# One level of Strassen for five float32 weight products, in two passes with the result in DRAM between

## The chip, the cores and the metric

One core of one Trainium2 chip. The metric is the time of one execution on the device in microseconds (us): 3072.22 before, the median of three runs (3071.91 to 3073.43). The clock given for a run is the mean granted TensorE clock of its profiled execution.

## The reference

Two graph layers over 128 graphs of 64 nodes with 768 features: 8192 rows, 64 tiles of 128 rows (two graphs each), all in float32. Cut to what matters:

```python
# layer 0: three weight products
h = relu(layernorm(x))
ctx = adj @ (h @ Wadj.T + badj) / deg + adj.T @ (h @ Wrev.T + brev) / rdeg + h @ Wself.T + bself
x = x + ctx + rel                 # rel: counts of relations, times small tables
# layer 1: two weight products, attention with 6 heads, a gate
h = relu(layernorm(x))
hw   = einsum('bni,hio->bhno', h, W)
attn = softmax(mask(leaky(src(tanh(hw)) + dst(tanh(hw)).T)))
feat = elu(attn @ hw + b)
gate = sigmoid(h @ H_w.T + H_b)
x = x + gate * feat + (1 - gate) * h
```

The five products with 768 x 768 weights, Wadj, Wrev, Wself, W and H_w, are nearly all of the arithmetic.

## The kernel before

One pass over the 64 tiles; layer 0 of tile t is interleaved with layer 1 of tile t - 1 and the attention of tile t - 2. The parts that the change replaces (cuts marked with `# ...`):

```python
    def stage_c(t):                                     # layer 0: three products in one PSUM sum
        # ...
        for s in (2, 0, 1):
            for kb in range(KB):                        # KB = 6 blocks of 128
                for hf in range(2):
                    nc.tensor.matmul(pc[:, hf, :HALF], S1T[t][:, kb, s, :],
                                     ws[s][:, kb, hf * HALF : (hf + 1) * HALF],
                                     start=(n == 0), stop=False)
        # ... counts times table, add to x, layernorm

    def stage_d(t):                                     # layer 1: two products
        # ... six transposes of h
        def product(w):
            p = psb.tile([P, 2, 512], F32, name="pb")
            for kb in range(KB):
                for hf in range(2):
                    nc.tensor.matmul(p[:, hf, :HALF], h1t[:, kb, :],
                                     w[:, kb, hf * HALF : (hf + 1) * HALF],
                                     start=(kb == 0), stop=(kb == KB - 1))
        ph = product(wh)
        # ... tanh on ScalarE; ph + bias on VectorE; two products with w_src, w_dst on GpSimd
        pg = product(wg)

    for t in range(NT + 2):
        # ...
        stage_e(t - 2)
        stage_c(t)
        stage_a(t + 1)
        stage_f(t - 2)
        # ...
        stage_d(t - 1)
```

Of the kernel before, what the change touches and what calls it, by code (L numbers as in the profile page):

```python
# [22 lines left out]
def kernel(  # L23
# [35 lines left out]

    nc = tc.nc  # L60
# [4 lines left out]
    KB = D // P  # L65
    H, DO = w_src.shape
# [3 lines left out]
    CT = 2  # L70
    NCH = NT // CT
# [3 lines left out]
    NROW = NCNT + 5  # L75
    W = DO + 1
    assert GT == 2 and N == 64 and DO == P and H == KB and NROW <= P and NT % CT == 0
# [5 lines left out]
    work = ctx.enter_context(tc.tile_pool(name="work", bufs=2))  # L83
    small = ctx.enter_context(tc.tile_pool(name="small", bufs=3))
    psb = ctx.enter_context(tc.tile_pool(name="psb", bufs=3, space=bass.MemoryType.PSUM))
    pss = ctx.enter_context(tc.tile_pool(name="pss", bufs=2, space=bass.MemoryType.PSUM))


    X, AI = {}, {}

    def load_x(t):
        if t < NT:
            X[t] = work.tile([P, D], F32, name="xt", bufs=4)
            nc.sync.dma_start(X[t], xf[t * P : (t + 1) * P, :])

    def load_adj(c):
        if c < NCH:
            AI[c] = work.tile([P, CT, 2, N], I32, name="ai", bufs=3)
            for d, src in ((0, adj), (1, adj_t)):
                nc.sync.dma_start(  # L100
                    AI[c][:, :, d, :],
                    src[c * CT * GT : (c + 1) * CT * GT].rearrange("(t g) i j -> (g i) t j", g=GT),
                )

    load_x(0)
    load_adj(0)
    load_x(1)


    ws = [const.tile([P, KB, D], F32, name=f"w{s}") for s in range(3)]  # L110
    wh = const.tile([P, KB, D], F32, name="wh")
    wg = const.tile([P, KB, D], F32, name="wg")
    tab = const.tile([NROW, D], F32, name="tab")
    bb = const.tile([P, DO], F32, name="bb")
    hbb = const.tile([P, D], F32, name="hbb")
    wsd = const.tile([P, 2, D], F32, name="wsd")
# [8 lines left out]
    et = const.tile([P, NREL], F32, name="et")  # L125
    nc.scalar.dma_start(et, e_t)
    wrt = work.tile([P, 2, D], F32, name="wrt", tag="s1", bufs=1)
    nc.scalar.dma_start(wrt[:, 0, :], wr_t)
    nc.scalar.dma_start(wrt[:, 1, :], wrr_t)
    for i, v in enumerate((br, brr, badj, brev, bself)):  # L130
        nc.scalar.dma_start(tab[NCNT + i : NCNT + i + 1, :], row(v, 1))
    for w, src in ((ws[2], wself_t), (ws[0], wadj_t), (ws[1], wrev_t), (wh, w_cat), (wg, hw_t)):
        for k in range(0, KB, 2):
            nc.scalar.dma_start(  # L134
                w[:, k : k + 2, :],
                src[k * P : (k + 2) * P, :].rearrange("(k p) n -> p k n", p=P),
            )
    nc.scalar.dma_start(bb, row(b_att, P))
    nc.scalar.dma_start(hbb, row(hb, P))
    nc.scalar.dma_start(wsd[:, 0, :], row(w_src, P))  # L140
    nc.scalar.dma_start(wsd[:, 1, :], row(w_dst, P))
# [9 lines left out]
    for g in range(GT):  # L151
# [3 lines left out]
    blkb = const.tile([P, P], BF16, name="blkb")  # L155
    nc.vector.tensor_copy(blkb, blk)
# [3 lines left out]
    vals = const.tile([P, NV, N], BF16, name="vals")  # L160
    nc.gpsimd.iota(vals, pattern=[[1, NV], [0, N]], base=1, channel_multiplier=0,
                   allow_small_or_imprecise_dtypes=True)
    rs_, pbds = [], []
    for i in range(2):
        a = const.tile([P, CT, 3, N], F32, name=f"r{i}")
        for k in range(CT):
            nc.vector.tensor_copy(a[:, k, 2, :], idc)
        rs_.append(a)
        p = const.tile([P, H, P], F32, name=f"pbd{i}")
        nc.gpsimd.memset(p, 0.0)  # L170
        pbds.append(p)


    ids = const.tile([P, NV], F32, name="ids")
    nc.gpsimd.iota(ids, pattern=[[1, NV]], base=1, channel_multiplier=0,
                   allow_small_or_imprecise_dtypes=True)
    es = const.tile([P, 2, NCNT], F32, name="es")
    nc.vector.memset(es, 0.0)
    for d in range(2):
        nc.vector.tensor_mul(es[:, d, d * NV : (d + 1) * NV],  # L180
                             et[:, d * NB + 1 : (d + 1) * NB], ids)
    pt = psb.tile([P, 2, 512], F32, name="pb")
    for hf in range(2):
        for d in range(2):
            nc.tensor.matmul(pt[:NCNT, hf, :HALF], es[:, d, :],
                             wrt[:, d, hf * HALF : (hf + 1) * HALF],
                             start=(d == 0), stop=(d == 1))
    nc.vector.tensor_copy(tab[:NCNT, :].rearrange("p (a b) -> p a b", a=2),
                          pt[:NCNT, :, :HALF])


    def norm_relu(src, name, bufs):

        st = small.tile([P, 2, 6], F32, name="st")
        for i in range(2):
            nc.vector.bn_stats(st[:, i, :], src[:, i * HALF : (i + 1) * HALF])  # L196
        mv = small.tile([P, 2], F32, name="mv")
        nc.vector.bn_aggr(mv, st.rearrange("p a b -> p (a b)"))
        ve = small.tile([P, 1], F32, name="ve")
        nc.vector.tensor_scalar(ve, mv[:, 1:2], EPS, None, op0=OP.add)  # L200
        rs = small.tile([P, 1], F32, name="rs")
        nc.gpsimd.tensor_tensor(rs, ve, mhalf, op=OP.pow)  # L202
        h = work.tile([P, D], F32, name=name, bufs=bufs)
        nc.vector.tensor_scalar(h, src, mv[:, 0:1], 0.0, op0=OP.subtract, op1=OP.max)
        nc.scalar.activation(h, h, AF.Copy, scale=rs)  # L205
        return h

    AB, CNT, RR = {}, {}, {}

    def prep_adj(c):  # L210

        if c >= NCH:
            return
        ai = AI[c]
        af = work.tile([P, CT, 2, N], F32, name="af", bufs=1)
        nc.vector.tensor_copy(af, ai)
        AB[c] = work.tile([P, CT, 2, N], BF16, name="ab")
        nc.gpsimd.tensor_copy(AB[c], af)
        cnt = CNT[c] = work.tile([P, CT, NROW], F32, name="cnt")
        nc.vector.tensor_reduce(cnt[:, :, NCNT : NCNT + 2], af, AX.X, OP.add)  # L220
        dc = small.tile([P, CT, 2], F32, name="dc")
        nc.vector.tensor_scalar(dc, cnt[:, :, NCNT : NCNT + 2], 1.0, None, op0=OP.max)
        rc = small.tile([P, CT, 2], F32, name="rc")
        nc.vector.reciprocal(rc, dc)
        nc.vector.tensor_mul(cnt[:, :, NCNT + 2 : NCNT + 4], cnt[:, :, NCNT : NCNT + 2], rc)
        nc.vector.memset(cnt[:, :, NCNT + 4 : NCNT + 5], 1.0)


        ds = pss.tile([P, CT, 2, N], F32, name="ps")
        nc.tensor.matmul(ds, blkb, AB[c], start=True, stop=True)  # L230
        rd = work.tile([P, CT, 2, N], F32, name="rd", bufs=1)
        nc.vector.tensor_scalar(rd, ds, 1.0, None, op0=OP.max)
        nc.vector.reciprocal(rd, rd)
        r = RR[c] = rs_[c % 2]
        for d in range(2):
            nc.vector.tensor_mul(r[:, :, 1 - d, :], af[:, :, d, :], rd[:, :, d, :])

    H0, CT_T, S1T, H1 = {}, {}, {}, {}
    HS, TG, SD, L, PB = {}, {}, {}, {}, {}

    def stage_a(t):

        if t >= NT:
            return
        c, k = divmod(t, CT)
        H0[t] = norm_relu(X[t], "h0", 1)
        for d in range(2):
            eq = work.tile([P, NV, N], BF16, name="eq", bufs=1)
            nc.vector.tensor_tensor(  # L249
                eq, AB[c][:, k, d, None, :].to_broadcast([P, NV, N]), vals, op=OP.is_equal)  # L250
            nc.vector.tensor_reduce(CNT[c][:, k, d * NV : (d + 1) * NV], eq, AX.X, OP.add)  # L251

    def stage_b(t):

        if t >= NT:
            return
        c, k = divmod(t, CT)
        pt = pss.tile([P, P], F32, name="ps")
        nc.tensor.transpose(pt[:NROW, :], CNT[c][:, k, :], ident)  # L259
        CT_T[t] = work.tile([NROW, P], F32, name="cntT")  # L260
        nc.scalar.copy(CT_T[t], pt[:NROW, :])

        s1 = S1T[t] = work.tile([P, KB, 3, P], F32, name="s1", bufs=1)
        for q in range(KB // 2):
            ps = psb.tile([P, GT, 512], F32, name="pb")
            for i in range(2):
                kb = 2 * q + i
                for g in range(GT):
# [3 lines left out]
                                     RR[c][s, k].rearrange("p s n -> p (s n)"),  # L272
# [5 lines left out]
    def stage_c(t):  # L278

        if t >= NT:  # L280
            return
        pc = psb.tile([P, 2, 512], F32, name="pb")
        n = 0
        for s in (2, 0, 1):
            for kb in range(KB):
# [12 lines left out]
    def stage_d(t):  # L298

        if not 0 <= t < NT:  # L300
            return
# [157 lines left out]
```

## Time and profile before

| | before |
|---|---|
| time | 3072.22 us |
| TensorE busy | 2977.0 us, 97% |
| VectorE, ScalarE, GpSimd busy | 58%, 20%, 18% |
| chain of work that ended last | TensorE 95% |
| one tile in the steady stretch | 46.90 us, so 93.80 us a pair of tiles |

The last row is the distance between the starts of the layer-0 products of two tiles in the timeline (1011.33 and 1058.23 us). The busy time of that stretch; the columns are the stretch, its length, then busy us and instructions of PE, PEld, DVE, ACT and POOL, the granted clock, the DMA share and GB/s:

```profile
1011.33:1058.23 46.90, 46.31 (x178) 28.62 (x176) 35.72 (x41) 9.41 (x16) 8.87 (x9) 1.00 0.06 20
```

TensorE hardly rests (46.31 us busy of 46.90); the next busiest, VectorE, has a quarter of its time free. The other lines of this profile are in the prediction.

### The profile page before, as it was taken

How to read it: one execution, taken by the hardware profiler on the slowest of the kernel's cores; microseconds unless marked ns; L12 is line 12 of the kernel's file. 1: busy time of each engine (PE TensorE's matmuls, PEld its weight loads, DVE VectorE, ACT ScalarE, POOL GpSimd, SP SyncE). 2: the span in 40 equal slices, each digit the busy share in tenths (PEclk: the TensorE clock that was granted, in tenths of full speed). 3: DMA queues.
4: the chain of work that ended last, by engine and by line, in shares of the span. 5: the costliest groups of instructions: out<-in, count | busy, mean ns of one | idle time of the engine just before them, and what ended most of it. 6: DMA issues, size and time to landing. Idle time of an engine off the chain costs nothing.

```text
span 3070.0 us, 27575 instructions
## 1 busy us (share of the span) xinstructions
PE 2977.0 (97%) x11240; PEld 1839.7 (60%) x11240; DVE 1773.2 (58%) x2319; ACT 602.4 (20%) x961; POOL 561.4 (18%) x554
## 2 busy tenths in 40 slices
PE   5999999999999999999999999999999999999997
PEld 3666666666666666666666666666666666666664
DVE  8266555576555665555765556655557655566334
ACT  1112121121121121211211211212112112112121
POOL 1112122121121121221211211212212112112111
PEclk7999999999999999999999999999999999999998
DMA  5000000000000000000000000000000000000000
GB/s 207 1 23 23 12 23 21 13 23 12 23 22 12 23 23 13 23 21 12 23 13 22 22 11 23 23 13 23 21 12 23 15 21 23 11 23 23 11 16 16
DMA packets 41064, 70.18 MB, mean 23 GB/s; under 512 B 19941, under 2 KB 20069, under 8 KB 40938
## 3 DMA queue, kind: packets, MB, share of 16 engines
q1 hardware_dynamic: 35840, 54.54, 5.4%
q10 hardware_dynamic: 5098, 13.89, 1.2%
q8 instruction: 88, 1.44, 0.2%
q14 instruction: 38, 0.31, 0.0%
HBM read 43.24 MB, written 25.17 MB: 22 GB/s over the span
## 4 chain that ended last, share of the span: by engine, by line
PE 95%; ACT 2%; DMA 1%; issue 1%; DVE 0%; ACTq 0%; POOL 0%
PE pb L287 48%; PE pb L314 33%; PE pb L270 5%; PE pb L380 3%; PE pb L292 3%; PE ps L352 2%; ACT pT L376 1%; ACT h1t L308 1%; PE ps L375 1%; PE ps L307 1%; DMA wh<-in_w_cat_dram 0%; ACTq L134 0%; PE ps L259 0%; PE ps L230 0%; DMA wrt<-in_wr_t_dram 0%
## 5 line engine op out<-in xcount | busy, mean ns | idle before, releaser
L287 PE MATMUL pb<-w,s 128*128 128x384 f32 x4608 | 1496.8, 486 | 0.0
L287 PEld LDWEIGHTS pb<-w,s 128*128 128x128 f32 x4608 | 875.4, 190 | 610.5 <-issue 0.4
L314 PE MATMUL pb<-wh,h1t 128*128 128x384 f32 x1536 | 512.4, 490 | 18.7 <-ACT h1t L308 18.7
L314 PE MATMUL pb<-wg,h1t 128*128 128x384 f32 x1536 | 505.8, 486 | 0.0
L295 DVE TENSOR_TENSOR xt<-pb,xt 128x768 f32<-128x768 f32 x64 | 61.3, 958 | 752.3 <-PE pb L292 752.2
L314 PEld LDWEIGHTS pb<-wh,h1t 128*128 128x128 f32 x1536 | 286.6, 190 | 220.4 <-ACT h1t L308 33.8
L314 PEld LDWEIGHTS pb<-wg,h1t 128*128 128x128 f32 x1536 | 291.8, 190 | 203.5
L251 DVE TENSOR_REDUCE cnt<-eq 128x39 f32<-128x2496 bf16 x128 | 352.4, 2753 | 2.2
L376 ACT COPY pT<-ps 128x384 f32<-128x384 f32 x128 | 55.2, 482 | 1244.7 <-PE ps L375 1244.5
L323 POOL MEMSET hs<- 128x6 f32 x64 | 7.3, 113 | 1327.7 <-PE pb L380 1327.7
L249 DVE TENSOR_TENSOR eq<-ab,vals 128x2496 bf16<-128x2496 bf16 x128 | 186.5, 1457 | 3.3
L331 POOL TENSOR_TENSOR pr<-th,wsd 128x768 f32<-128x768 f32 x64 | 116.0, 1813 | 365.9 <-ACT th L321 365.9
L270 PE MATMUL pb<-r,h 64*128 64x192 f32 x1536 | 145.1, 336 | 7.5 <-ACT h L205 7.5
L270 PEld LDWEIGHTS pb<-r,h 64*128 64x128 f32 x1536 | 126.2, 190 | 31.0 <-issue 22.9
L274 ACT COPY s<-pb 128x768 f32<-128x768 f32 x192 | 140.0, 799 | 3.5 <-PE pb L270 3.5
L337 DVE TENSOR_TENSOR tg<-pb,hbb 128x768 f32<-128x768 f32 x64 | 61.3, 958 | 134.5 <-PE pb L314 134.5
L357 POOL MEMSET lm<- 128x384 f32 x64 | 26.7, 417 | 578.1 <-ACT pbd L365 578.1
L196 DVE BATCH_NORM_STATS2 st<-xt 128x6 f32<-128x384 f32 x256 | 127.2, 539 | 2.9 <-DMA xt<-in_x_dram 0.7
L202 POOL TENSOR_TENSOR rs<-ve,mhalf 128x1 f32<-128x1 f32 x128 | 107.6, 851 | 89.4 <-DVE ve L200 89.2
L380 PE MATMUL pb<-hs,pT 128*128 128x129 f32 x768 | 105.0, 287 | 18.6 <-ACT pT L376 18.6
L389 DVE TENSOR_SCALAR e<-f 128x768 f32<-128x768 f32 x64 | 120.7, 1886 | 2.2
L205 ACT ACTIVATE h<-h,rs 128x768 f32<-128x768 f32 x128 | 113.2, 931 | 44.2 <-POOL rs L202 44.1
(70 smaller groups left out, 2090.8 us busy)
## 6 DMA issues: line engine op xcount, KB each, us to landing
xt<-in_x_dram SPq DMA_DIRECT2D x64, 384.0 KB, 3.2
out_dram<-f SPq DMA_DIRECT2D x64, 384.0 KB, 2.6
w<-in_wself_t_dram ACTq DMA_DIRECT2D x3, 768.0 KB, 9.7
w<-in_wadj_t_dram ACTq DMA_DIRECT2D x3, 768.0 KB, 13.1
w<-in_wrev_t_dram ACTq DMA_DIRECT2D x3, 768.0 KB, 14.7
wh<-in_w_cat_dram ACTq DMA_DIRECT2D x3, 768.0 KB, 15.0
wg<-in_hw_t_dram ACTq DMA_DIRECT2D x3, 768.0 KB, 15.4
ai<-in_adj_dram SPq DMA_DIRECT2D x32, 64.0 KB, 1.9
```

The lines of the kernel that those rows point to most:

```text
L196: nc.vector.bn_stats(st[:, i, :], src[:, i * HALF : (i + 1) * HALF])
L202: nc.gpsimd.tensor_tensor(rs, ve, mhalf, op=OP.pow)
L205: nc.scalar.activation(h, h, AF.Copy, scale=rs)
L249: nc.vector.tensor_tensor(eq, AB[c][:, k, d, None, :].to_broadcast([P, NV, N]), vals, op=OP.is_equal)
L251: nc.vector.tensor_reduce(CNT[c][:, k, d * NV : (d + 1) * NV], eq, AX.X, OP.add)
L270: nc.tensor.matmul(ps[:, g, i * 3 * N : (i + 1) * 3 * N], H0[t][s, kb * P : (kb + 1) * P], RR[c][s, k].rearrange("p s n -> p (s n)"), star ...
L274: nc.scalar.copy(s1[:, 2 * q : 2 * q + 2].rearrange("p i s (g n) -> p g (i s) n", g=GT), ps[:, :, : 6 * N].rearrange("p g (x n) -> p g x n ...
L287: nc.tensor.matmul(pc[:, hf, :HALF], S1T[t][:, kb, s, :], ws[s][:, kb, hf * HALF : (hf + 1) * HALF], start=(n == 0), stop=False)
L314: nc.tensor.matmul(p[:, hf, :HALF], h1t[:, kb, :], w[:, kb, hf * HALF : (hf + 1) * HALF], start=(kb == 0), stop=(kb == KB - 1))
L331: nc.gpsimd.tensor_mul(to, th, wsd[:, s, :])
L380: nc.tensor.matmul(po[:, b, i * W : (i + 1) * W], pT[:, h, :], HS[t][:, h, :], start=True, stop=True)
L389: nc.vector.tensor_scalar(e, f, 0.0, None, op0=OP.min)
```

## The change

Strassen's algorithm multiplies two 2 x 2 block matrices with 7 block products in place of 8. Here the two tiles of a pair are the block rows, the halves of 768 the block columns. A pair needs 63 matmuls of 128x384 in layer 0 (72 before) and 42 in layer 1 (48 before). In return, sums of operand blocks (S1 to S4) are made on VectorE and GpSimd, and each result block collects several products by adds. The seven products are called P1 to P7. The sums of weights are kept in SBUF, where the kernel has its tiles, one layer's at a time; so layer 0 runs over all pairs first, writes its result to DRAM, and layer 1 runs after it. The intent was less work for the engine that bounds the kernel. The table product became bf16 in three parts in the same change. Names that recur below: h is a tile's normalised rows; pr and th are GpSimd's products for the attention logits and dg its last operand for them; PSUM, in tiles that the kernel calls banks, is where its products' sums stand until another engine reads them. Core of the diff, long parts cut:

```diff
-    work = ctx.enter_context(tc.tile_pool(name="work", bufs=2))
+    X1 = [dram.tile([2 * P, D], F32, name=f"x1_{p}") for p in range(NP)]
 ...
-        for s in (2, 0, 1):
-            for kb in range(KB):
-                for hf in range(2):
-                    nc.tensor.matmul(pc[:, hf, :HALF], S1T[t][:, kb, s, :], ...
+            mm("a", lambda: A1[p][:, :, 0], "11", True)
+            add(x0, 0, "a")
+            mm("c", lambda: A1[p][:, :, 1], "21", True)
+            counts("c", 0, 0)
+            add(x0, 0, "c")
+            mm("b", lambda: S1[p], "T1", True)
+            add(x1, 1, "b")
+            mm("a", lambda: S2[p], "T2", False)
+            add(x0, 1, "a")
+            mm("d", lambda: A22[p], "T4", True)
+            ...
+            mm("a", lambda: S3[p], "T3", False)
+            ...
+            mm("b", lambda: S4[p], "22", False)
 ... second pass
+        def norm(t):
+            h = H1[t] = work.tile([P, D], F32, name="h1", bufs=6)
+            nc.scalar.activation(h, X[t], AF.Relu, scale=mv1[:, t, 0:1], bias=mv1[:, t, 1:2])
+                    if s == 0:
+                        nc.scalar.copy(part(t, s, q), sums(b, s))        # P1, P5, P6, P4: copy on ScalarE
+        def add(t, s, q, b):
+                nc.vector.tensor_add(part(t, s, q), sums(b, s), part(t, s, q))
+        def gate(t):
+            ...
+            nc.gpsimd.tensor_add(HS[t][:, :, :DO], HS[t][:, :, :DO],     # bias, on VectorE before
+                                 bb[:, None, :].to_broadcast([P, H, DO]))
+            nc.gpsimd.tensor_add(X[t], X[t], H1[t])
+        def final(t):
+            ...
+            nc.gpsimd.tensor_sub(e, e, H1[t])
+            nc.vector.scalar_tensor_tensor(f, f, 0.0, e, op0=OP.max, op1=OP.add)
+            nc.vector.scalar_tensor_tensor(f, f, -1.0, Z[t], op0=OP.add, op1=OP.mult)
+            nc.vector.tensor_add(f, f, X[t])
+        for p in range(NP):
+            merged(main(p), before(p + 1) + behind(p - 1))               # 42 products, side steps between
```

## The prediction

> **What bounds the kernel now.** I read the page of the kernel before from the top: busy shares, chain, groups; then the busy time by stretches, the timeline of one steady tile and the one of the last tiles.
>
> ```profile
> PE 2977.0 (97%) x11240; PEld 1839.7 (60%) x11240; DVE 1773.2 (58%) x2319; ACT 602.4 (20%) x961; POOL 561.4 (18%) x554
> ...
> PE 95%; ACT 2%; DMA 1%; issue 1%; DVE 0%; ACTq 0%; POOL 0%
> ...
> L287 PE MATMUL pb<-w,s 128*128 128x384 f32 x4608 | 1496.8, 486 | 0.0
> ...
> L314 PE MATMUL pb<-wh,h1t 128*128 128x384 f32 x1536 | 512.4, 490 | 18.7 <-ACT h1t L308 18.7
> L314 PE MATMUL pb<-wg,h1t 128*128 128x384 f32 x1536 | 505.8, 486 | 0.0
> ```
>
> TensorE bounds it: 97% busy, 95% of the chain of work that ended last. The five weight products are 2304 + 1536 matmuls of 128x384, each recorded twice (4608, 2 x 1536), and take 1496.8 + 512.4 + 505.8 = 2515 us: 0.65 us each, 39 us of the 47 us per tile. So removing a matmul shortens the kernel, as long as the others keep up.
>
> ```profile
> 0.00:40.00 40.00, 8.15 (x20) 3.90 (x22) 36.65 (x54) 2.53 (x4) 9.29 (x17) 0.72 0.95 351
> ...
> 1000.00:2000.00 1000.00, 987.57 (x3753) 610.43 (x3752) 598.91 (x775) 200.99 (x321) 186.73 (x182) 1.00 0.06 19
> ```
>
> Busy time by stretches (columns: length, then PE, PEld, DVE, ACT, POOL busy). The first 40 us are start (weights at 351 GB/s, VectorE full); later PE is busy 987.57 of 1000. The full clock (1.00) is granted there.
>
> The costs I need for VectorE and GpSimd are in the groups and timelines:
>
> ```profile
> L251 DVE TENSOR_REDUCE cnt<-eq 128x39 f32<-128x2496 bf16 x128 | 352.4, 2753 | 2.2
> L249 DVE TENSOR_TENSOR eq<-ab,vals 128x2496 bf16<-128x2496 bf16 x128 | 186.5, 1457 | 3.3
> ...
> L331 POOL TENSOR_TENSOR pr<-th,wsd 128x768 f32<-128x768 f32 x64 | 116.0, 1813 | 365.9 <-ACT th L321 365.9
> ```
>
> ```profile
> 1041.08 1.81 POOL L391 TENSOR_TENSOR xt<-xt,h 128x768 f32<-128x768 f32 x1 [0.21 <-ACT h L205]
> 1041.36 1.95 DVE L389 TENSOR_SCALAR e<-f 128x768 f32<-128x768 f32 x1
> ...
> 3009.58 1.87 POOL L391 TENSOR_TENSOR xt<-xt,h 128x768 f32<-128x768 f32 x1 [1.08 <-ACT h L205]
> ...
> 3010.75 1.51 DVE L393 SCALAR_TENSOR_TENSOR f<-f,e 128x768 f32<-128x768 f32 x1 [0.97 <-ACT e L390]
> 3012.30 0.96 DVE L394 SCALAR_TENSOR_TENSOR f<-f,h 128x768 f32<-128x768 f32 x1
> ```
>
> Timeline columns: start, duration. The first VectorE op takes 1.95 us beside GpSimd; alone at the kernel's end it takes 0.56. The second, with two SBUF inputs, takes 1.51 against 0.96: it ends at 3012.26, 0.81 us after GpSimd ended at 3011.45.[...]
>
> [...]
>
> **The change, part by part.** The unit is a pair of tiles (32 pairs).
>
> *Removed.* Strassen takes 7 block products for 8: layer 0 has 3 x 7 x 3 = 63 matmuls per pair for 72, layer 1 has 42 for 48. 15 x 0.65 = 9.75 us a pair, 312 us in all. The table products become 8 bf16 matmuls (1.3 us) for 4 float32 ones (93.2/32 = 2.9 us): another 1.6 us a pair, 51 us, less about 10 for split transposes.
>
> *TensorE floor.* Layer 0 per pair: 63 x 0.65 = 41.0; operands 2 x 145.1/64 = 4.5; table 1.3; the rest 0.8: 47.6 us. Layer 1: 42 x 0.65 = 27.3; transposes 2 x 1.68 = 3.4; attention 2 x 1.64 = 3.3; the block product 1.4: 35.4 us. 32 x 83.0 = 2656 us, against 2977 busy now. If the rest hid, start and ends of some 110 us would give about 2770.
>
> *But the other engines now have the same work in less time, each stage with its own share*[...]. So I took the compiled order of each engine's instructions for one steady pair and added up durations from the groups.
>
> *Layer 0.* VectorE, from the last add of a pair: that add and the statistics 3.7 (of it some 1.9 waiting for GpSimd's power, which it now needs back), two statistics 1.0, degrees 0.4, reciprocal 1.75, add 0.55, r 0.5, conversions and statistics 2.8, then the four comparisons and counts 4 x (1.46 + 2.75) = 16.8, mixed with two adds (1.1) and small ones (1.1), and only then S3 and S1 of the next pair's first block (1.1). With gaps of 0.03 us that is about 31.7 us. The third block of operands can start on TensorE only when those two have freed a PSUM buffer (two buffers for all operands); TensorE gets there at 28.4 us. It waits some 3.3 us, and nothing gives it back, since the next pair starts from the same add: 47.6 + 3.3 = 50.9 us.
>
> *Layer 1.* GpSimd has, per pair, 12 operations of 1.81 us (four products for the logits, bias, x + h, e - h), two of 0.83, two sums of 0.9 and small ones: 22.6 of 35.4 us. VectorE 25 us, of which 9.2 have two SBUF inputs[...]. From the end of the first half's last product (P3): VectorE's final step of an older tile[...] (3.0), the add (0.55), tanh (0.9), then on GpSimd pr, h + b, th, h + b, pr, th, e - h at 1.81 and dg 0.85, with one VectorE op between (0.9): dg lands at about 18.9. TensorE wants it at 14.4: 4.5 us. Then the logits' PSUM is read only at 25.2, after VectorE operations that wait for GpSimd in turn, and the next transpose, which needs that buffer, waits 2.3 more. 35.4 + 6.8 = 42.2 us.[...]
>
> *Start, seam, end.* In pair 0, VectorE has counts, weight sums (9 x 1.26, contending with 8 us on GpSimd) and the table ahead; the table's matmul stops TensorE until about 80, and pair 0 ends near 112. Layer 1's first loads wait for all engines of pass 0, since the memory is used again: 4.7 MB at 351 GB/s are 13 us, sums after, so P5 starts some 25 us late. The last pair leaves logits, softmax and final steps, some 40 us.
>
> *Sum.* 112 + 30 x 50.9 + 43 (last pair, without preparations) + 25 + 25 (rest of layer 1's first pair) + 31 x 42.2 + 40 = 3080. The gain of 320 us goes to waits: 99 in layer 0, 210 in layer 1, the rest at start and seam.
>
> **The rivals.** (a) *TensorE remains the bound*, about 2770 to 2850: for it speaks the 70% mean load of VectorE in both passes, banks with one or two products between write and reuse, and the evident trouble taken over placing the steps. Against it speaks the compiled order: side steps don't stand where their numbers put them; the four counts come together, ahead of S3 and S1. (b) *The waits hold in layer 0[...]*: 38 us in layer 1, 3080 - 130 = 2950. Against it is the pair of timeline rows above, if only one of many operations. (c) *Worse*:[...] layer 1 takes 44 to 45 us: 3150. (d) *DRAM between the passes*: 50 MB more traffic, at the 384 KB in 3.2 us of the issues listed, prefetched: hidden; only the seam is paid.
>
> **Range and chances.** The sum is 3080. Ledgers of this kind count each wait once and fully, and (a) and (b) lie only below; I say 3055, range 2900 to 3160. Faster means under 3011, which needs (b) or most of (a): 0.33. Within 2% (3011 to 3134): 0.48. Slower: 0.19, from (c) and a longer start.
>
> **What would show it.** TensorE busy about 2650 us, some 86% of the span. Products of layer 0 (63 a pair) and layer 1 (42 a pair) at 0.65 us each. A pair every 51 us in the first half; PE's waits there name the third operand block, released by VectorE. In the second half a pair every 42 us, VectorE ops of 0.96 us lasting up to 2.7 us, PE waiting for dg and then for the logits' reader. A seam of some 25 us with an idle TensorE. I am wrong if TensorE is above 92% busy, if layer 1's pairs take under 38 us, or if the second half's two-input operations keep their 0.96 us.

The cut passages (marked) named mechanisms and figures that no run of this case shows; they stood behind my estimate of how much longer operations of VectorE and GpSimd get beside each other. No term of the sums goes with them: 35.4 + 6.8 = 42.2 us for layer 1 and 3080 us in all are as recorded. Only the reason for the 3.0 us of VectorE's final step is gone, and that the same sum came to 38 us without this lengthening. That is rival (b), lengthening that costs little; (c) is more of it. The 1.3 us for eight bf16 table products was an estimate, and the trace of the kernel after shows it: two take 0.33 us of TensorE's stream (650.53 to 650.86), so eight 1.32.

## The result, and the profile after

3037.38 us, the median of four runs (3035.43 to 3038.00), against 3072.82 us of the kernel before on the same chip. The ratio is 0.9884, 95% interval 0.9867 to 0.9901: 1.2% less, by the rule of 2% the same. (Ratios are the mean time of one kernel's fast runs over that of the other's of the same rounds, so not quite the ratio of the medians quoted.) The mean granted TensorE clock fell from 0.992 to 0.956. The result is correct.

TensorE lost 237 us of work (2977.0 to 2740.4), and the kernel only 35. The page of the kernel after, busy shares and chain:

```profile
PE 2740.4 (90%) x10360; PEld 1638.6 (54%) x10360; DVE 1970.5 (65%) x2999; ACT 752.5 (25%) x1251; POOL 1170.5 (39%) x1021
...
PE 40%; POOL 24%; DVE 19%; issue 11%; DMA 3%; ACT 3%; SPq 0%; ACTq 0%; POOLq 0%; DVEq 0%
```

GpSimd's work doubled, and what ended last hung on TensorE for 40% only. Three stretches: a pair of layer 0, the seam between the passes with the first pair of layer 1, a pair of layer 1 (columns as above):

```profile
613.90:663.30 49.40, 48.99 (x189) 28.32 (x188) 31.99 (x50) 6.75 (x12) 10.32 (x13) 1.00 0.11 35
...
1647.60:1715.10 67.50, 35.80 (x110) 21.50 (x110) 25.95 (x33) 12.38 (x19) 29.39 (x24) 0.75 0.41 144
2166.40:2207.70 41.30, 35.77 (x137) 22.47 (x136) 27.81 (x43) 16.68 (x27) 24.49 (x19) 0.92 0.12 40
```

Layer 0 is bound by TensorE: 48.99 of 49.40 us. Layer 1 isn't: 35.77 of 41.30, and its clock is 0.92. The waits of TensorE by name (us in total, times, longest):

```profile
PE pma L560 <- ACT hs L585: 160.7, 29, 5.9
PE pb L332 <- DVE s L352: 31.2, 30, 12.5
PE ps L531 <- DMA x<-x: 24.1, 1, 24.1
```

One wait makes up nearly all of layer 1's loss: 29 times 5.5 us, product P6 for ScalarE's copy of P1, which frees the PSUM bank that both use. The timeline of one steady pair shows why the copy is late (start, duration; in brackets idle time and what ended it):

```profile
2206.04 2.52 POOL L638 TENSOR_TENSOR pr<-th,wsd 128x768 f32<-128x768 f32 x1
2206.93 2.45 DVE L708 TENSOR_TENSOR f<-f,x 128x768 f32<-128x768 f32 x1
2207.69 2.10 PE L560 MATMUL pma<-bv,a 128*128 128x384 f32 x6
2208.52 2.43 POOL L649 TENSOR_TENSOR hs<-hs,bb 128x768 f32<-128x768 f32 x1
...
2212.69 1.74 POOL L649 TENSOR_TENSOR hs<-hs,bb 128x768 f32<-128x768 f32 x1
...
2218.07 1.80 POOL L705 TENSOR_TENSOR e<-e,h 128x768 f32<-128x768 f32 x1
...
2219.91 1.03 ACT L524 ACTIVATE h<-x,mv 128x768 f32<-128x768 f32 x1 [5.45 <-POOL e L705]
2220.84 0.46 ACT L585 COPY hs<-pma 128x384 f32<-128x384 f32 x1
...
2221.44 1.62 PE L560 MATMUL pma<-bvT,s 128*128 128x384 f32 x2 [5.52 <-ACT hs L585]
```

Read it from below. TensorE stood 5.52 us for the copy at 2220.84. The copy's input, P1, was there since 2209.79; yet ScalarE stood idle for 5.45 us and ran the copy only behind the normalisation h at 2219.91, which stood ahead of it and waited for GpSimd's e - h: the new h reuses the buffer which that operation reads. And e - h came last of seven long GpSimd operations in a row, from 2206.04 to 2219.87. So the wait called "copy of P1" is GpSimd's queue. The waits' view alone names ScalarE, which is 25% busy.

The matmuls after the wait take 1.62 us for two records, which take 0.81 elsewhere: from 2221.44 to 2225.00 the granted clock is 0.50, and in the stretch above it is 0.92. Where the same wait is only 2.23 us (next section, e2) the two records take 0.88. But in e6 (next section) two records take 1.49 us soon after a wait of only 2.01 us. So in these runs the length of the wait alone doesn't decide; what else does, no run shows.

Groups that answer to those of the prediction (busy, mean ns of one | idle before):

```profile
L308 DVE TENSOR_REDUCE cnt<-eq 128x39 bf16<-128x2496 bf16 x128 | 351.5, 2746 | 2.0
L638 POOL TENSOR_TENSOR pr<-th,wsd 128x768 f32<-128x768 f32 x64 | 138.2, 2159 | 13.5 <-ACT th L634 13.5
L649 POOL TENSOR_TENSOR hs<-hs,bb 128x768 f32<-128x768 f32 x64 | 131.0, 2047 | 0.0
L707 DVE SCALAR_TENSOR_TENSOR f<-f,z 128x768 f32<-128x768 f32 x64 | 124.7, 1949 | 0.1
L708 DVE TENSOR_TENSOR f<-f,x 128x768 f32<-128x768 f32 x64 | 110.8, 1731 | 0.1
```

The counts cost what they did. Two-input VectorE operations, 0.96 us in the kernel before, now average 1.95 and 1.73, and the GpSimd ones that meet them 2.05 to 2.16 for 1.81. In the timeline above both sides last longest where they overlap (2.45 beside 2.52 and 2.43 us): these collisions are real, as predicted; why they take time, no run shows.

### The profile page after: what moved, and what is told of

The parts are those of the page before. It is cut to its first block, busy times and chain, and to the rows that moved or that the text cites. A ratio compares the mean times of both kernels' runs of the same rounds, so it can differ in the third digit from the quotient of the medians.

```text
span 3035.0 us, 27842 instructions
## 1 busy us (share of the span) xinstructions
PE 2740.4 (90%) x10360; PEld 1638.6 (54%) x10360; DVE 1970.5 (65%) x2999; ACT 752.5 (25%) x1251; POOL 1170.5 (39%) x1021
## 3 DMA queue, kind: packets, MB, share of 16 engines
q8 instruction: 82, 1.34, 0.2%
## 4 chain that ended last, share of the span: by engine, by line
PE 40%; POOL 24%; DVE 19%; issue 11%; DMA 3%; ACT 3%; SPq 0%; ACTq 0%; POOLq 0%; DVEq 0%
PE pwa L376 8%; PE pma L560 7%; PE pwb L376 7%; PE pwd L376 6%; DVE cnt L308 5%; POOL pr L638 4%; POOL hs L649 4%; DVE eq L305 4%; POOL th L638 4%; POOL e L705 4%; PE pmc L560 4%; POOL s L362 2%; DVE st L142 2%; POOL rn L147 2%; POOL x L651 2%
## 5 line engine op out<-in xcount | busy, mean ns | idle before, releaser
L560 PE MATMUL pma<-bvT,s 128*128 128x384 f32 x768 | 331.6, 545 | 160.7 <-ACT hs L585 160.7
L376 PE MATMUL pwa<-bwT,s 128*128 128x384 f32 x1152 | 401.5, 493 | 0.0
L308 DVE TENSOR_REDUCE cnt<-eq 128x39 bf16<-128x2496 bf16 x128 | 351.5, 2746 | 2.0
L376 PEld LDWEIGHTS pwa<-bwT,s 128*128 128x128 f32 x1152 | 210.7, 190 | 141.6 <-issue 19.4
L332 PE MATMUL pb<-r,h 64*128 64x192 f32 x1536 | 178.6, 351 | 49.6 <-DVE s L352 31.2
L376 PE MATMUL pwb<-bwT,s 128*128 128x384 f32 x576 | 216.7, 505 | 0.0
L376 PE MATMUL pwb<-bw,s 128*128 128x384 f32 x576 | 201.3, 492 | 0.0
L376 PE MATMUL pwd<-bwT,a 128*128 128x384 f32 x576 | 201.2, 495 | 0.0
L376 PE MATMUL pwa<-bw,a 128*128 128x384 f32 x576 | 196.6, 489 | 0.0
L376 PE MATMUL pwc<-bw,a 128*128 128x384 f32 x576 | 191.0, 486 | 0.0
L560 PE MATMUL pmb<-bvT,s 128*128 128x384 f32 x384 | 146.6, 492 | 7.0 <-DVE s L545 7.0
```

Of the source, the lines that this page charges most:

```text
L308: nc.vector.tensor_reduce(CNT[p][:, k, d * NV : (d + 1) * NV], eq, AX.X, OP.add)
L332: nc.tensor.matmul(ps[:, g, i * 3 * N : (i + 1) * 3 * N], H0[t][s, kb * P : (kb + 1) * P], rts[p % 2][s, k].rearrange("p s n -> p (s n)"), ...
L376: nc.tensor.matmul(bank[b][:, :HALF], a()[:, q, s, :], bw[w][:, q, s, :], start=(first and q == s == 0), stop=(q == KH - 1 and s == 2), sk ...
L560: nc.tensor.matmul(bank[b, s][:, :HALF], a[p][:, q, :], bw[w][:, q, s, :], start=(first and q == 0), stop=(q == KH - 1), skip_group_check= ...
```

## The experiments

Four explanations of layer 1's 41.3 us a pair: (A) too few h buffers, (B) the length of GpSimd's queue, (C) the collisions, the longer durations of VectorE's and GpSimd's operations beside each other, (D) TensorE's own work. And one question beyond: what Strassen itself gives, and what the two passes cost. All runs were timed in three rounds (4 runs of each changed kernel; the kernel before took 3072.7 to 3073.1 us in each session); the pair is the mean distance of layer 1's pairs in the timeline over some 25 pairs. In the kernel after most pairs take 41.3 us and some 42.5, so the mean is 41.7. Classes follow the rule of 2%: the kernel after and e1 are the same as the kernel before, e6 is unclear, e7 to e9 are slower, the others faster.

| run | edit | us | ratio to before | pair of layer 1 | clock |
|---|---|---|---|---|---|
| after | | 3037.38 | 0.9884 | 41.7 | 0.956 |
| e1 | 8 h buffers | 3029.65 | 0.9861 | 41.4 | 0.969 |
| e2 | no bias add | 2924.55 | 0.9515 | 38.0 | 0.977 |
| e3 | bias add replaced by a free fill | 2953.89 | 0.9616 | 38.0 (steady) | 0.973 |
| e4 | e1, and bias on VectorE | 2977.27 | 0.9687 | 39.8 | 0.966 |
| e5 | bias add replaced by bound fills | 2971.76 | 0.9668 | 39.3 | 0.966 |
| e6 | bias on VectorE | 3015.02 | 0.9810 | 41.0 | 0.956 |
| e7 | layer 1 without Strassen | 3157.05 | 1.0274 | 45.7 | 0.965 |
| e8 | layer 0 without Strassen | 3194.56 | 1.0397 | 41.6 | 0.958 |
| e9 | neither with Strassen | 3314.40 | 1.0785 | 45.7 | 0.968 |
| e10 | second tile's heads earlier | 2987.55 | 0.9718 | 40.1 | 0.980 |
| e11 | e10 and e6 | 2949.97 | 0.9603 | 39.0 | 0.978 |
| e12 | e11 and 8 h buffers | 2937.36 | 0.9557 | 38.7 | 0.979 |

**e1: more h buffers.**

```diff
-            h = H1[t] = work.tile([P, D], F32, name="h1", bufs=6)
+            h = H1[t] = work.tile([P, D], F32, name="h1", bufs=8)
-            e = work.tile([P, D], F32, name="e")
+            e = work.tile([P, D], F32, name="e", bufs=1)
```

> Eight buffers for the normalised rows of layer 1 instead of six (and one instead of two for the exponentials, to make room). The changed kernel takes 3037 us and 41.3 us a pair in layer 1; TensorE waits 5.5 us a pair for ScalarE's copy of product P1, which stands behind a normalisation that waits for GpSimd (e - h) to give back a buffer. Theory A, the buffer count is the cause: the wait goes, 35.5 to 36.5 us a pair, 2860 to 2890 us. Theory B, GpSimd's chain to dg is the cause and the buffer only the place where it shows: the wait moves to dg, which lands 1.8 us sooner because one x + h leaves its way: 39 to 40 us a pair, 2965 to 3000 us, PE waiting for POOL dg.

3029.65 us (3028.17 to 3031.57): 8 us less. The wait that the trace of the kernel after names is gone, and others took its place:

```profile
PE ps L658 <- POOL dg L642: 104.9, 33, 11.8
PE ps L531 <- ACT a L542: 61.5, 29, 2.8
```

The buffer through which GpSimd's lateness reached TensorE was not its cause. A is out. B's forecast had the place right, dg, and the gain wrong: 8 us instead of 37 to 72.

**e2: no bias add.** The bias is zero in these inputs, so the result stays correct; this is an experiment and no kernel to keep.

```diff
-            nc.gpsimd.tensor_add(HS[t][:, :, :DO], HS[t][:, :, :DO],
-                                 bb[:, None, :].to_broadcast([P, H, DO]))
```

> GpSimd's two additions of the attention bias per pair are dropped (the bias is zero in these inputs, so the result stays right; in general it would be wrong). GpSimd loses 3.6 of 24.7 busy us a pair. Theory B (GpSimd's chain sets the pair): the pair falls by 3.6 us or a bit more[...]: 36 to 37.7 us, 2875 to 2925 us. If the buffer count, the evacuations or TensorE set it: within 0.5 us of 41.3, 3020 to 3040 us.

(The reason for the "bit more" is cut; no run shows it as a rule.)

2924.55 us (2920.22 to 2926.81), just within B's forecast, the pair (38.0) just above it: 113 us less for 64 operations of some 2 us on an engine that is 39% busy. The same place in the timeline:

```profile
2206.04 2.52 POOL L638 TENSOR_TENSOR pr<-th,wsd 128x768 f32<-128x768 f32 x1
...
2208.65 2.42 POOL L638 TENSOR_TENSOR th<-th,wsd 128x768 f32<-128x768 f32 x1
...
2214.76 1.81 POOL L703 TENSOR_TENSOR e<-e,h 128x768 f32<-128x768 f32 x1
...
2216.60 1.03 ACT L524 ACTIVATE h<-x,mv 128x768 f32<-128x768 f32 x1 [2.14 <-POOL e L703]
2217.53 0.46 ACT L585 COPY hs<-pma 128x384 f32<-128x384 f32 x1
...
2218.14 0.88 PE L560 MATMUL pma<-bvT,s 128*128 128x384 f32 x2 [2.23 <-ACT hs L585]
```

From the first product to the end of e - h GpSimd needs 10.53 us instead of 13.83: 3.30 less, and this pair is as much shorter (38.04 us for 41.34, from one first product to the next). TensorE's wait falls by 3.29. So GpSimd's work in that chain sets the pair, microsecond for microsecond. Whether by its time or by the collisions, the time alone doesn't say; the line at 2208.65 is taken up under e5.

**e3: a fill in place of the add.** A write of the same engine that reads nothing, meant to be about as long (it took 1.48 us, for 1.74 to 2.43 of the add; with one e buffer, as in e1, to make room for it).

```diff
-            nc.gpsimd.tensor_add(HS[t][:, :, :DO], HS[t][:, :, :DO],
-                                 bb[:, None, :].to_broadcast([P, H, DO]))
+            nc.gpsimd.memset(scr, 0.0)          # scr: 128 x 1660, read by nobody
```

> The same two additions are replaced by memsets of about the same length (1660 elements, some 1.8 us), which read no SBUF. GpSimd keeps its time[...]. If only GpSimd's time counts: 3025 to 3045 us, as the changed kernel. If [...] (VectorE's L706 to L708 last 1.25 to 1.95 us for 0.96): the pair falls by 1 to 2 us, 2975 to 3005 us.

(The cut clauses rest on a cause of the collisions that no run shows; the second forecast is for C as a large part.)

2953.89 us (2951.41 to 2960.16), 84 us less than after and below both forecasts. I first took this as the collisions' share of e2's gain. It isn't: the run failed as an experiment, as one line on the fill shows (duration min/median/max in ns, first and last start):

```profile
L651 POOL MEMSET scr<- x64: 1472/1482/1490, 1656.9 to 1814.8; 128x1660 f32 x64
```

The fill depended on nothing, so the scheduler moved all 64 to the start of layer 1. The steady pairs have none and last 38.0 us, as e2's; the 29 us between e2 and e3 are lost at the start.

**e4: e1 with the bias on VectorE.** The bias joins the multiplication that reads the attention's PSUM, as the reference has it.

```diff
-            nc.vector.tensor_mul(FF[t][...], po[:, :, :DO], ri.to_broadcast([P, HH, DO]))
+            for i in range(HH):
+                h = q * HH + i
+                nc.vector.scalar_tensor_tensor(FF[t][:, h * DO : (h + 1) * DO], po[:, i, :DO],
+                                               ri[:, i, :], bb, op0=OP.mult, op1=OP.add)
```

> Eight buffers as in the first run, and the bias is added by VectorE where it reads the attention out of PSUM (three operations of 128x128 with one SBUF input in place of one of 128x384), so that GpSimd no longer has it; right for any bias. VectorE gains about 1 us a pair. Theory B: dg lands 3.6 us sooner again, waits of 0 to 1.5 us are left, 35.5 to 37 us a pair, 2860 to 2905 us, some 5 to 7% under the kernel before. If VectorE is now the limit: 38 us or more a pair, above 2935 us.

2977.27 us (2974.17 to 2978.32): a miss for theory B; the other forecast (above 2935) came. TensorE's waits were for VectorE's read of the logits (67.5 us) and ScalarE's copy of a transposed block (45.4 us).

**e5: the fill again, bound to its place.**

```diff
-            nc.gpsimd.tensor_add(HS[t][:, :, :DO], HS[t][:, :, :DO], ...
+            nc.gpsimd.memset(HS[t][:, :, :DO], 0.0)
+            nc.gpsimd.memset(HS[t][:, :, :DO], 0.0)
+            nc.gpsimd.memset(HS[t][:, :HH, :DO], 0.0)
```

> Repeats the question of e3 properly. In e3 the write-only fill depended on nothing, and its profile shows all 64 fills between 1656.9 and 1814.8 us, ahead of the steady pairs; its pairs then last 38.02 us, as those without any bias add do (38.04)[...]. Here GpSimd fills the attention's own head tile (128x768 twice and 128x384, wrong result on purpose) where the bias add stood, so it can't move forward; each fill costs about 0.9 ns an element of a row, so about 1.8 us a tile. If [...]: pair of layer 1 at 38.0 to 38.9 us, 2925 to 2955 us in all. If it was GpSimd's time in the chain to the buffer of h: pair at 40.3 to 41.4 us, 3000 to 3040 us.

(Cut as in e3: the first forecast is for C.)

2971.76 us (2963.84 to 2975.00). Its output is wrong, which doesn't matter for the time. The pair, 39.3 us, lies between the two forecasts. The timeline decides: of six fills, 2.60 us stood ahead of e - h (three of 0.73, one of 0.41), the others slipped behind it, and the chain from the first product (2222.99) to the end of this operation took 12.04 us:

```profile
2233.23 1.80 POOL L706 TENSOR_TENSOR e<-e,h 128x768 f32<-128x768 f32 x1
```

| | chain on GpSimd, us | pair, us |
|---|---|---|
| after | 13.83 | 41.7 |
| e5 | 12.04 | 39.3 |
| e2 | 10.53 | 38.0 |

Chain and pair shrink together. The bias add costs its time in the chain, B. One of the two adds took 2.43 us for the other's 1.74, 0.7 us that I put down to the collision with VectorE; but e2 did not gain even that, for there the next operation meets VectorE in its place (th, 2.42 us at 2208.65, for 1.83 before). What e2 gained, 3.30 us, is about twice the 1.74 of an undisturbed add. The rest of C stays untested: no run removed the collisions and left the work.

**e6: bias on VectorE, six h buffers** (the edit of e4 without that of e1).

> The bias add goes from GpSimd to VectorE (three fused 128x128 multiply-adds at the attention's PSUM read in place of one 128x384 multiply), h keeps its six buffers; right for any bias. If GpSimd's chain sets the pace: 2925 to 2945 us, close to e2's 2924.6, TensorE's waits again at the copy of P1 (2 to 3 us a pair). If VectorE has no room: 2970 or more, as in e4.

3015.02 us (3011.66 to 3016.28): 70 us above the first forecast, and the reason given with the second (VectorE full) isn't it either. GpSimd's chain is short now (10.93 us), yet the pair is 41.0. The compiled order moved: ScalarE's copy of P1 stands ahead of the late normalisation, and the next copies (a, of transposed blocks) behind it; TensorE comes to the logits' product before dg is there. Waits between 1900 and 2800 us:

```profile
PE ps L656 <- POOL dg L642: 44.2, 22, 2.0
PE ps L531 <- ACT a L542: 15.2, 22, 0.9
PE ps L531 <- ACT a L538: 13.9, 22, 0.7
PE ps L531 <- DVE a L658: 11.5, 22, 1.6
```

Four short waits in place of a long one, 3.9 us a pair together, and the slow clock with them (0.956 over the run). The longest is 2.01 us, before which TensorE was busy without a gap for over 9 us; yet soon after it two records take 1.49 us for 0.81 and four (at 2219.25) 2.77 for 1.45, and from 1800 to 2400 the granted clock is 0.91:

```profile
2214.80 0.91 PE L656 MATMUL ps<-dg,blk 128*128 128x384 f32 x2 [2.01 <-POOL dg L642]
...
2217.97 1.49 PE L560 MATMUL pma<-bvT,s 128*128 128x384 f32 x2
```

So TensorE's own work takes 37.1 us a pair here (815.26 us busy in the 900 from 1900), 35.7 in the kernel after (782.47). That the changed order is the cause of these waits is read from the timeline; no run put the order back.

**e7, e8, e9: Strassen taken out, layer by layer.** The two passes, the DRAM trip and the side steps with their places stay; the block products are summed in PSUM as in the kernel before. The same edit is made in layer 0 (e8), layer 1 (e7) and both (e9); e7's core:

```diff
-            for f, s in ((p1, 0), (p2, 0), (p5, 0), (p1, 1), ...          # 42 products
+            for s in range(2):                                            # 48 products
+                for k, t in ((0, t0), (1, t1)):
+                    for q in range(2):
+                        # ... choice of the bank b, n
+                        mm((b, n), s, (A11, A21)[k], ("11", "T3")[q], True)
+                        mm((b, n), s, (A12, A22)[k], ("21", "22")[q], False)
-                nc.vector.tensor_sub(new(S3, "s3"), A11[p], ps)           # and S1, S2, S4
+                nc.scalar.copy(new(A21, "a21"), ps)
```

> Layer 1 without Strassen (48 products of 128x384 a pair in place of 42, no sums S, 8 evacuations in place of 18); layer 0 keeps it. If Strassen's saving in layer 1 is lost in the waits of the side work, as I hold: TensorE's own work is about 39 us a pair, the pair 38.5 to 41.3 us, the whole 2945 to 3037 us, no slower than with Strassen. If layer 1 were bound by TensorE: 6 x 0.49 us more a pair, minus 2 us at most elsewhere, and so 3070 to 3130 us.

> Layer 0 without Strassen (96 products of 128x384 a pair in place of 84, no sums S); layer 1 keeps it. If layer 0 is bound by TensorE: 12 x 0.486 = 5.8 us more a pair less the four operand products and waits that become cheaper, 5.0 to 5.8 us, 32 times: 3195 to 3225 us. If VectorE held layer 0 back as the prediction said (3.3 us a pair): only 2 to 2.5 us more a pair, 3100 to 3120 us.

> Both layers without Strassen, the two passes and the round trip through DRAM kept: what the passes alone cost. e8 (layer 0 without) is 157 us over the changed kernel, e7 (layer 1 without) 120 us. If the savings of the two layers add up and all that is left is the price of two passes: 3037 + 157 + 120 = 3314 us, 240 us over the kernel before. If e7 was slow for reasons of its own (a schedule not fitted to it) and the passes cost little: that can't be told from this run alone, but then its pairs of layer 1 must show more waiting than the 5.5 us of the changed kernel. If the two passes were nearly free, as the small seam suggests: 3120 to 3180 us.

3157.05, 3194.56 and 3314.40 us. Two forecasts have an error in their arithmetic: a product takes 0.65 us of TensorE's stream (two records), not the 0.49 us that one record lasts (six in a row take 2.10), and layer 0 has 72 and 63 products a pair, not 96 and 84. In e8's forecast the two errors cancel (12 x 0.486 = 5.8 = 9 x 0.65); that it was met to 0.5 us (3195 to 3225) is luck to that extent. Rightly, e7 would add 6 x 0.65 = 3.9 us a pair, 121 in 31 pairs, if all of it arrived; it added 120. I had expected none of it to arrive, since layer 1 waits anyway. That was wrong, and the result is above both forecasts: TensorE waits as long as before, 5.5 us a pair in the 900 us from 1900 (5.4 in the kernel after), though the wait for the copy of P1 is gone and waits in the attention have come. Why the new waits add up to the old, no run shows. In layer 0, 9 x 0.65 = 5.8 us could arrive, and 5.2 a pair did (54.62 against 49.45). e9 hit the sum:

- Strassen in layer 0 saves 3194.56 - 3037.38 = 157 us with Strassen in layer 1, and 3314.40 - 3157.05 = 157 without.
- Strassen in layer 1 saves 3157.05 - 3037.38 = 120 us with Strassen in layer 0, and 3314.40 - 3194.56 = 120 without.
- All else in the change, which is the two passes with the new side work, less what the cheaper table product saves, costs 3314 - 3073 = 241 us. No run takes these apart.

So 277 us gained, 241 given back, 36 left. Where the 241 lie: in e9 a pair takes 54.62 us in layer 0 (173.98 - 119.36 in these lines) and 45.7 in layer 1, together 6.5 more than the 93.80 of before, 202 us in 31 pairs; the other 40 I put down to the seam and the start, which this run doesn't separate.

```profile
119.36 4.03 PE L358 MATMUL pwa<-bw,a 128*128 128x384 f32 x12
...
173.98 4.04 PE L358 MATMUL pwa<-bw,a 128*128 128x384 f32 x12
```

And TensorE's waits in e9's layer 1, all on the side work of the attention:

```profile
PE ps L600 <- DVE f L615: 116.7, 32, 3.8
PE ps L600 <- ACT pbd L591: 33.8, 32, 5.7
PE ps L612 <- ACT pT L601: 24.6, 31, 0.8
```

In the 900 us from 1900 they make 5.2 us a pair, nearly as much as in the kernel after but under other names. In the one-pass kernel TensorE stands for only 1.2 us a pair (twice 46.90 - 46.31). So of the 6.5 us more a pair, 4.0 are waits. In the other 2.5 TensorE is busier: the operand products take 178.2 us for 145.1 in all, and the clock in layer 1 is 0.95. The waits I read so: in one pass the products of layer 0 fill the time in which layer 1's side chains run, and the separation took that filling away. That is a reading of the traces; no run put layer 0's products back between. And e7 and e9 use the side steps' places made for 42 products, so their waits, and with them the split of 120 and 241, belong to this schedule.

**e10: the second tile's heads earlier.** Its sums are complete at product 31 of its own pair; until now its tanh and GpSimd products started with the next pair, together with those of the first tile.

```diff
-                    (3, lambda: heads(t1)),
+        def own(p):
+            return [(31, lambda: heads(2 * p + 1))]
 # and the second tile goes first through gate, softmax and attention
-            merged(main(p), before(p + 1) + behind(p - 1))
+            merged(main(p), before(p + 1) + behind(p - 1) + own(p))
```

> GpSimd's work spread instead of removed: the second tile's heads (tanh, two products on GpSimd, dg) start at product 31 of the pair's own 42, where that tile's sums are complete, in place of product 3 of the next pair; the second tile then goes first through the softmax. The same instructions[...]. If the wait for the copy of P1 comes from GpSimd's pile-up of some 14 us at the seam of two pairs: it falls from 5.5 us to below 2.5 us, pair 37 to 39.5 us, 2910 to 2985 us. If it is the sum of GpSimd's work[...]: 40.5 us or more, 3010 or more.

2987.55 us (2982.13 to 2988.80), 50 us less with not one instruction removed. The wait for the copy of P1 fell from 160.7 to 13.7 us; what is left is 57.1 us for a copy of a transposed block and 45.5 for a VectorE add. So the pile-up was a good part of it; though the total (2987.55, forecast up to 2985) and the pair (40.1, up to 39.5) lie just above the forecast for it.

**e11: e10 and e6 together.**

> As e10, and the bias add on VectorE as in e6. If pile-up and amount of GpSimd's work add up: pair 36.5 to 38.5 us, 2890 to 2955 us, the fastest right version so far. If VectorE is then what is late: no better than e10.

2949.97 us (2944.49 to 2953.68), correct for any bias and within the forecast, though the pair (39.0) is above it. With the heads spread, the bias on VectorE gains 38 us, where alone it had gained 22.

**e12: and eight h buffers.**

> e11 with eight h buffers (one e buffer), as e1 had: in e11's steady pair TensorE stands 2.66 us for ScalarE's copy of a transposed block, which stands behind the normalisation that waits for GpSimd's e - h and its buffer; with eight buffers the normalisations run a pair ahead. If that buffer is what is left to wait for: 1.5 to 2.5 us less a pair, 2870 to 2905 us. If, as in e1, the wait only changes its name (x + h is now behind both dg's, and VectorE waits for it): 2935 to 2965 us.

2937.36 us (2934.34 to 2941.20), correct for any bias: 13 us less than e11. The forecast of the wait changing its name was the right one; the largest are now these two:

```profile
PE ps L531 <- ACT a L542: 75.6, 29, 3.2
PE ps L531 <- DVE a L658: 33.7, 28, 1.2
```

This is the fastest correct version: ratio 0.9557 to the kernel before (interval 0.9541 to 0.9573), and 0.9557 / 0.9884 = 0.967 to the kernel after. Its pair, 38.7 us, is still 2.9 above the 35.8 us for which TensorE was busy in a pair of the kernel after.

## Why the prediction was right or wrong

The class and the range were right, and that most of the gain would not arrive; the change in time was -17 us forecast and -35 measured. The step that failed is layer 0's wait of 3.3 us for VectorE, which measured 0.4 us; in layer 1 the size of the waits was about right (6.8 us a pair forecast, 5.5 measured) and their path wrong. The 3055 was not the sum either but the sum of 3080 lowered by judgement. The terms, in us:

| term | predicted | measured |
|---|---|---|
| start and pair 0 | 112 | 122.1 |
| 30 pairs of layer 0 | 30 x 50.9 = 1527 | 30 x 49.45 = 1483.4 |
| last pair | 43 | 42.1 |
| seam, rest of layer 1's first pair | 25 + 25 | 67.4 |
| 31 pairs of layer 1 | 31 x 42.2 = 1308 | 31 x 41.3 = 1280.2 |
| tail | 40 | 39.7 |
| sum | 3080 (said: 3055) | 3034.9 |

**TensorE floor, layer 0.** 47.6 predicted, 49.0 measured, because small products set between large ones are dear. In the timeline of the pair at 613.90 six groups of four operand products (8 records) each take 0.85 us plus about 0.1 at either side, 1.05 for the 0.75 assumed. This error and the next have opposite signs, 1.4 us a pair against 2.9, so that the total of layer 0 looks better than its parts.

**"It waits some 3.3 us, and nothing gives it back."** This step failed. The wait is there, at the third block of operands and for VectorE, as said, but it is 0.4 us in the steady pair at 613.90 (31.2 us in all, 12.5 of it in the first):

```profile
614.43 0.56 DVE L393 TENSOR_TENSOR x<-pwb,x 128x384 f32<-128x384 f32 x1 [1.98 <-PE pwb L385]
...
643.66 0.55 DVE L352 TENSOR_TENSOR s<-a,pb 128x384 f32<-128x384 f32 x1
...
644.36 0.92 PE L332 MATMUL pb<-r,h 64*128 64x192 f32 x8 [0.41 <-DVE s L352]
```

Counted from the last add, at 614.43, VectorE has freed the buffer after 29.8 us (31.7 forecast), and TensorE comes to it after 29.5 (28.4 forecast; the floor again). So 1.9 us of VectorE's queue were counted too much and 1.1 of TensorE's too little. e8 agrees that TensorE bounds layer 0: nine more products a pair cost 5.2 us, nearly all of their TensorE time.

**Layer 1.** 42.2 against 41.3 looks right, and is half luck. TensorE's work (35.4) was right to 0.4. GpSimd's sequence with the two bias adds was the one found (its "12 operations of 1.81 us" are 10; the sum of 22.6 us is that of 10, and 24.5 were measured), and the two-input VectorE operations went up to 2.45 us (2.7 said). But the waits named were wrong: "4.5 us" for dg and 2.3 for the logits' reader, where the trace has 17.0 us in all for dg and 160.7 for the copy of P1. I had followed the data to the logits and not the buffer: e - h holds an h buffer, the normalisation waits for it, and ScalarE's queue passes that on. That the same sum gives 38 us without the collisions (rival b) is not shown: 38.0 us came with two operations fewer, the collisions still there (2.45 us for VectorE's f + x at 2206.94 in e2's timeline). The lower clock (0.92 in the pair above) was not in the sum at all.

**Seam.** 50 predicted, 67.4 measured. The wait for the first load was as forecast, 24.1 us for 25; the rest of the first pair took 43.3 us for 25. In it TensorE waits 7.0 us for VectorE's sums, and its first matmuls are at half the pace (six records 4.03 us, 2.10 later). **Start** was 10 us longer; the weight sums, contending as said, took 1.34 us each on VectorE (1.26 said) and 17.8 us on GpSimd (8 said), where one lasted 12.56 us and the shortest 2.62.

**The rivals.** (a) holds for layer 0 and fails for layer 1. (b) had the wrong reason; its 38 us a pair were reached by shortening GpSimd's chain. (c) didn't come. (d) holds: the DMA share in layer 1 is 0.12, and TensorE waits for a load only at the seam.

The prediction's frame was too narrow in one thing: it asked which engine would bind after the change, and not what the one-pass interleaving had been worth. Of the 241 us given back, the 4.0 us of waits a pair, some 124 in all, are what I put down to its loss; and moving side work and buffers about won back 3 of a pair's 41.7 us (e12) without undoing the two passes, so even these are not the price of the separation as such. The hint was in the profile before: TensorE was busy 46.31 of 46.90 us although the side chains of layer 1 were there too, because it always had the other layer's products to go on with.

## What to carry to other kernels

Before splitting a pass that interleaves two stages, add up what each stage's side chain needs alone: the split can expose latencies that the other stage's work had covered. Here 241 of the 277 us gained were given back, about half of it as such waits, by my reading. When the wait list names a little-used engine, look at what stands ahead of the named operation in its queue, and follow buffers as well as data. Spread a slow engine's work over the period before moving it to another engine, and check in the trace that an experiment's substitute stayed where it was put.
